# A megakernel of two conv/scan layers: loads at the head of each stage, empty half units behind them, and one more in each turn of the chunk scan

## The chip, the cores and the metric

The kernel runs on one core of one Trainium2 chip, as one launch with one instruction stream per engine: PE (TensorE, matmuls), DVE (VectorE), ACT (ScalarE), POOL (GpSimd) and SP (SyncE, which here issues every DMA). The metric is device time in microseconds. The time of the kernel before is the median of three runs.

## The reference

Eight images of 64 x 64 tokens with 192 channels go through two layers, all in float32. Cut to what matters:

```python
# layer 0 (INNER=384, K=2 directions, N=32 states, 12 heads of 64)
xl, z = split(x @ W_in.T)                      # 384 + 384 channels
xc = silu(depthwise3x3(xl) + conv_b)
BCdt = x_proj(xc in row order, xc in column order)
dt = softplus(dt + dt_bias); da = exp(dt * A)
h = da_t * h + dt_t * x_t * B_t ; y_t = h . C_t       # over 4096 tokens, twice
y = y0 + y1 (turned back), + Ds * x
out = x + (y * silu(z)) @ W_out.T
x1 = out + silu(out @ W1.T + b1) @ W2.T + b2
# layer 1 (halves of 96 channels; inner 192, 16 states, 4 directions)
left  = relu(conv1x1(relu(bn(conv3x3(relu(bn(conv3x3(bn(xl)))))))))
u = silu(depthwise3x3(in_proj(layernorm(xr)))); four orders of the tokens
delta = softplus(dt_proj(x_dbl)); A = -exp(A_logs)
h = exp(delta_t * A) * h + delta_t * u_t * B_t ; y_t = h . C_t   # 4 directions
right = out_proj(layernorm(sum of directions + Ds * u) * silu(z))
out = interleave(left, right) + x1
```

## The kernel before

**The main sequence.** Layer 1's scan (`selective_scan`) is the backbone. A unit is one [128 x 1024] block: eight channels of one direction with their 16 states on the partitions, and 1024 tokens along the free axis. There are 3072 units, 384 per image: 8 steps of 3 tiles of 16 units. For each unit SP fetches the decays into `dA` (`fetch`, L1390, four units ahead, in five buffers, so a fetch waits until the scan five units back has let its buffer go), ACT takes the exponent (`decay`, L1395), PE spreads the inputs into PSUM (`spread`, L1403), the DVE multiplies by B (`weigh`, L1418) and scans (L1425), POOL multiplies by C (L1429), ACT keeps the last column (`carry_on`, L1435 and L1436), and every fourth unit PE sums over the states (`gather`, L1447). `prepare` computes the next tile's softplus and its inputs in pieces over the 16 units, with ACT, POOL and several DMAs (`dld`, `dud`, `dus`, L1359 to L1381).

**The work beside it.** Everything else runs as Python generators beside the scan: `conv0`, `ssd` and `mlp0` are layer 0 of the next image; `conv_branch`, with `scan_sums` as its side, and `scan_outputs` finish the image before; `scan_inputs` and `transposed` prepare layer 1's scan of the next image. `stages` lists them when an image's loop starts, at the ninth unit of the second tile in the last step of the image before.

**The order of the instructions.** All engines take their instructions in program order (`pin`), which the emitter fixes by a credit rule (class `Beside`). A unit has two halves. In each half `Beside.half` adds the rate to the credit (what is left over counts up to one more rate), and then emits pieces of the first stage in the list. A piece ends with `yield cost`, and the cost is taken off the credit; at zero the half is over. A piece that ends with `yield None` ends the half at once, whatever the credit. The costs of the stages are what their pieces yielded when the first image went through before the loop (`finish`, without the scan and without pacing), apart from two that are written down:

```python
self.rate = (own + sum(self.costs.get(gen.__name__, 40.0) for gen in self.stages)) / halves
```

`own` is 450 and `halves` is 768 for a whole image. What is left in the list when the loop of an image ends is emitted in one lump by `finish`. The side of `conv_branch` moves in every half up to its next `None`, without credit.

**The stages that the change touches.** Each stage opens its own SBUF pools when it starts and issues its first loads there. `conv0` loads its weights and x, sets three pads to zero on POOL (L371), then projects, convolves and, in `turn`, transposes into `xo` (ACT copy L440) and projects into `po`, which SP stores to `xrows` and `prows` (L461). `ssd` is the chunked scan of layer 0: `group` loads B, C and dt of eight chunks from `prows` (L512, L513) and computes their decays on POOL (L520), ACT and PE; then 32 chunks go through `fetch`, `decays` (PE turns B and C into `ps_t`, L586, and ACT copies them to `bc`, L591), `weigh`, `outputs` (the DVE adds to `Hm`, L639; POOL makes `Hn`, L641; the DVE adds to `Hn`, L654; PE multiplies `ps_y`, L664) and `store`, one stage per chunk and turn, oldest chunk first (`in_turn`). `mlp0` loads y from `yrows`, gates, projects and runs the MLP over blocks of 512 tokens. `conv_branch`, `scan_inputs` and `scan_outputs` run over blocks of 512 tokens through `in_turn`, too, with a load as the first stage. `scan_sums` adds up the directions: a whole [128 x 4096] tile, then blocks, each loaded a block ahead. `transposed` writes the turned copy of `u`.

Of the kernel before, what the change touches and what calls it, by code (L numbers as in the profile page):

```python
# [18 lines left out]
PW = WW + 2  # L19
# [269 lines left out]

def in_turn(items, *stages):  # L290
# [64 lines left out]
def conv0(cx, x):  # L355
# [3 lines left out]
    with cx.pool("cw0") as wp, cx.pool("v0", 2) as vp:  # L359
        w_in = load_split(cx, wp, "w_in", k["p0_w_in"][:, :INNER0], INNER0)  # L360
        diag = wp.tile([128, NJ, 9, 64], F32, tag="diag", name="diag")
        pin(nc.sync.dma_start(out=diag, in_=k["diag0"]))
        xp = wp.tile([128, 2 * NJ, 2 * NP0], F32, tag="xp0", name="xp0")
        for i in range(2):
            pin(nc.sync.dma_start(
                out=xp[64 * i : 64 * (i + 1)], in_=k["p0_xp"].rearrange("(j p) k m -> p j (k m)", p=64)
            ))

        pads = [wp.tile([128, R2 + 2, PW], F32, tag=f"pad{j}", name=f"pad{j}") for j in range(NJ)]
        for j in range(NJ):  # L370
            pin(nc.gpsimd.memset(pads[j], 0.0))  # L371
# [59 lines left out]
        def turn(p, q):  # L431

            here = slice(q * 128, (q + 1) * 128)
            xo = vp.tile([128, 2, INNER0], F32, tag="xo", name="xo")
# [27 lines left out]

        load(0)
        for j in range(NJ):
            yield from project(0, j)
        load(1)
# [13 lines left out]
def ssd(cx):  # L480
# [15 lines left out]
    with cx.pool("g0", 2) as gp, cx.pool("s0", 2) as sp:  # L496
# [63 lines left out]
        for _ in coming:  # L560
            yield 0.3
# [14 lines left out]
        def decays(c):  # L576
# [12 lines left out]
            yield 0.6  # L589
            bc = sp.tile([2 * N0, 2, Q], F32, tag="bc", name="bc")  # L590
# [35 lines left out]
        def outputs(c):  # L626
# [25 lines left out]
            yield 0.9  # L652
            ps = pss[1].rearrange("p (h c) -> p h c", c=HP)
            pin(nc.vector.tensor_add(Hn, ps, Hn))  # L654
            yield None
# [37 lines left out]
def mlp0(cx, x, x1):  # L693
# [9 lines left out]
    with cx.pool("mw0") as wp, cx.pool("m0", 2) as mp:  # L703
        w_z = load_split(cx, wp, "w_z", k["p0_w_in"][:, INNER0:], INNER0)
        w1 = load_split(cx, wp, "w1", k["p0_w1"], HID)
        w_out = wp.tile([128, NJ, C], F32, tag="w_out", name="w_out")
        pin(nc.sync.dma_start(out=w_out, in_=k["p0_w_out"].rearrange("(j p) m -> p j m", p=128)))
        w2 = wp.tile([128, NF, C], F32, tag="w2", name="w2")
        pin(nc.sync.dma_start(out=w2, in_=k["p0_w2"].rearrange("(f p) m -> p f m", p=128)))
# [120 lines left out]
        load_x(0)  # L830
        load_y(0)
        for i in range(NI + 1):
# [16 lines left out]
def conv_branch(cx, xl, short, out, side=None):  # L849

    nc, pin, k = cx.nc, cx.pin, cx.k
    with cx.pool("cw1") as wp, cx.pool("a1", 2) as ap:
        ws = []
        for n in ("conv1_w", "conv2_w"):
            w = wp.tile([CH, 9, CH], F32, tag=n, name=n)
            pin(nc.sync.dma_start(out=w, in_=k[n]))
            ws.append(w)
# [822 lines left out]
```

## Time and profile before

| | us |
|---|---|
| median of three runs (17870.95 to 17890.11) | 17880.6 |
| profiled execution, its own time | 17927.61 |
| its span from the first to the last instruction | 17925.8 |
| busy: PE, DVE, POOL, ACT | 13953, 12239, 12013, 10436 |
| first and last scan of the main sequence | 934.9 and 17692.4 |
| loop of an image (the third with all seven stages) | 2178 |

The profile lists groups of instructions by line: engine, operation, tiles, shape and count, then busy time, the mean of one in ns, and the idle time of that engine just before them with what ended it. The view of the waits gives, for a pair of a waiting instruction and the one that released it, the total in us, the number of times and the longest. The timeline shows instructions in order of time: start, duration, engine, line, and in brackets the idle time before. The view by windows gives busy times in a stretch. Granted clock is the share of full speed at which PE was clocked.

### The profile page before, as it was taken

Reading aid. Unit: us, or ns where it says so; the run is one execution under the profiler, and the core shown is the slowest. Engines: PE = TensorE matmul, PEld = TensorE weight load, DVE = VectorE, ACT = ScalarE, POOL = GpSimd, SP = SyncE. Lnnn points to the kernel's source line nnn. Section 1 sums busy time; section 2 is a strip of 40 time slices with the busy share of each in tenths; the row PEclk is TensorE's granted clock in tenths of the full one; section 3 lists DMA queues with packets and bytes.
Section 4 is the critical chain, followed back from the end, with each engine's and each line's share of the span. In section 5 each row is a group of like instructions: output and inputs, shape, how many; then the busy total and the mean of one; then the engine's idle time right before and its main releaser. Section 6 shows DMA issues by size and latency. Waiting matters only on the chain. (4 is left out here: it accounts for less than half of the span.)

```text
span 17925.8 us, 221564 instructions
## 1 busy us (share of the span) xinstructions
PE 13953.2 (78%) x75752; PEld 4910.9 (27%) x75752; DVE 12239.1 (68%) x9264; ACT 10435.9 (58%) x18285; POOL 12013.0 (67%) x6437
## 2 busy tenths in 40 slices
PE   8877787778877787778877788777887777878776
PEld 4423322332123321233213332133322333211111
DVE  2177777676777767677567775677756777667884
ACT  2364576465664656647566475654756547555664
POOL 4168766775668756687567865677756786567784
PEclk9987788788787887878878788787977778877676
DMA  3376777677776777767777677777777767778785
GB/s 89 95 195 168 181 187 207 163 194 185 180 202 162 199 189 176 193 171 196 186 187 187 172 196 186 186 182 177 194 182 189 183 179 196 178 199 202 193 204 142
DMA packets 1584062, 3241.99 MB, mean 181 GB/s; under 512 B 387465, under 2 KB 834073, under 8 KB 1579353
## 3 DMA queue, kind: packets, MB, share of 16 engines
q1 hardware_dynamic: 1582936, 3227.82, 70.8%
q8 instruction: 605, 9.91, 0.2%
q14 instruction: 521, 4.26, 0.1%
HBM read 2548.91 MB, written 678.18 MB: 180 GB/s over the span
## 5 line engine op out<-in xcount | busy, mean ns | idle before, releaser
L1429 POOL TENSOR_TENSOR h<-h,bc 128x1023 f32<-128x1023 f32 x3072 | 7229.4, 2357 | 4209.2 <-DVE h L1425 3592.1
L1425 DVE TENSOR_TENSOR_SCAN h<-dA,carry,dB 128x1024 f32<-128x1024 f32 x3072 | 7198.0, 2343 | 594.0 <-ACT dA L1395 187.3
L1418 DVE TENSOR_TENSOR dB<-dB,bc 128x1024 f32<-128x1024 f32 x3072 | 3741.6, 1218 | 3133.2 <-PE dB L1403 3126.0
L1395 ACT ACTIVATE dA<-dA,neg_a 128x1024 f32<-128x1024 f32 x3072 | 3487.5, 1135 | 746.1 <-DMA dA<-dld 743.5
L1447 PE MATMUL acc<-h,gather 128*32 128x512 f32 x12288 | 2476.9, 749 | 733.0 <-ACT h L1436 235.9
L1403 PE MATMUL dB<-dus,spread 24*128 24x512 bf16 x6144 | 1364.2, 432 | 437.9 <-DVE h L1425 340.0
L1452 ACT COPY y<-acc 128x512 f32<-128x512 f32 x1536 | 871.7, 576 | 1227.1 <-PE acc L1447 1225.0
L868 PE MATMUL ps_c<-p,conv_w 96*96 96x512 f32 x2304 | 1294.9, 690 | 116.3 <-ACT p L889 105.3
L1403 PEld LDWEIGHTS <-spread 24*128 24x128 bf16 x6144 | 308.0, 94 | 2682.5 <-issue 1645.6
L1436 ACT ACTIVATE h<-h,bc 128x1 f32<-128x1 f32 x3072 | 905.4, 295 | 162.6 <-ACT carry L1435 2.2
L664 PE MATMUL ps_y<-dtx,M 64*64 64x64 f32 x12288 | 758.1, 253 | 298.5 <-DVE Hn L654 291.1
L1435 ACT COPY carry<-h 128x1 f32<-128x1 f32 x3072 | 573.9, 187 | 600.7 <-DVE h L1425 598.0
L325 PE MATMUL ps_cv<-pad,diag 64*64 64x512 f32 x6912 | 847.1, 607 | 31.0 <-ACT xc L428 30.5
L1447 PEld LDWEIGHTS acc<-h,gather 128*32 128x32 f32 x12288 | 323.1, 118 | 1850.3 <-issue 929.4
L664 PEld LDWEIGHTS ps_y<-dtx,M 64*64 64x64 f32 x12288 | 635.8, 165 | 491.1 <-issue 259.7
L596 PE MATMUL ps_d<-R,after 128*128 128x384 f32 x1024 | 627.3, 706 | 111.1 <-DVE M L621 54.1
L1349 POOL TENSOR_TENSOR w<-w,e 128x1024 f32<-128x1024 f32 x192 | 452.5, 2357 | 284.0 <-ACT carry L1435 195.4
L868 PEld LDWEIGHTS ps_c<-p,conv_w 96*96 96x96 f32 x2304 | 374.9, 182 | 855.7 <-issue 717.6
L350 PE MATMUL ps_h<-oa,w1a 128*128 128x256 f32 x1536 | 483.0, 438 | 159.1 <-ACT h L810 90.0
L591 ACT COPY bc<-ps_t 64x256 f32<-64x256 f32 x256 | 93.4, 365 | 728.6 <-PE ps_t L586 726.3
L779 PE MATMUL ps_m<-h,w 128*128 128x512 f32 x768 | 436.2, 710 | 78.3 <-DVE gT L774 36.8
L654 DVE TENSOR_TENSOR Hn<-ps_s,Hn 64x384 f32<-64x384 f32 x256 | 139.9, 546 | 518.8 <-POOL Hn L641 510.2
(258 smaller groups left out, 22143.6 us busy)
## 6 DMA issues: line engine op xcount, KB each, us to landing
dA<-dld SPq DMA_DIRECT2D x3072, 512.0 KB
dud<-terms SPq DMA_DIRECT2D x192, 768.0 KB
dus<-dud SPq DMA_DIRECT2D x2304, 64.0 KB
bc<-bcd SPq DMA_DIRECT2D x256, 512.0 KB
y<-yrows SPq DMA_DIRECT2D x256, 384.0 KB
u<-u SPq DMA_DIRECT2D x192, 512.0 KB
dld<-dl SPq DMA_DIRECT2D x192, 512.0 KB
y<-y SPq DMA_DIRECT2D x3072, 32.0 KB
```

Of the source, the lines that this page charges most:

```text
L325: pin(nc.tensor.matmul(ps[64 * b : 64 * (b + 1)].rearrange("p (h w) -> p h w", w=WW), lhsT=diag[:, t, :], rhs=pad[64 * i : 64 * (i + 1), b ...
L596: pin(nc.tensor.matmul(ps, lhsT=k["after"], rhs=flat(R[:, d * NH : (d + 1) * NH, :]), start=True, stop=False))
L664: pin(nc.tensor.matmul(psy[d][here, h * HP : (h + 1) * HP], lhsT=M[here, d, h, :], rhs=dtx[here, d, h, :], start=True, stop=d == 1,))
L868: pin(nc.tensor.matmul(ps.rearrange("p (h w) -> p h w", w=WW), lhsT=w[:, t, :], rhs=pad[:, dy : dy + RB, dx : dx + WW], start=t == 0, stop ...
L1395: pin(nc.scalar.activation(dAs[q], dAs[q], AF.Exp, scale=k["neg_a"][:, steps[m][1], t, i : i + 1]))
L1403: pin(nc.tensor.matmul(dBs[q][:, half, :], lhsT=k["spread"][at : at + 3 * UD, :], rhs=du_of[n][at : at + 3 * UD, i // 2, :], start=True, s ...
L1418: pin(nc.vector.tensor_mul(dBs[q], dBs[q], of(q)[0]))
L1425: pin(nc.vector.tensor_tensor_scan(order(h, g), order(dA, g), order(dB, g), carry, ALU.mult, ALU.add))
L1429: pin(nc.gpsimd.tensor_mul(h[:, rest], h[:, rest], C_[:, rest]))
L1436: pin(nc.scalar.activation(end, end, AF.Identity, scale=C_[:, last : last + 1]))
L1447: pin(nc.tensor.matmul(ps[32 * v : 32 * (v + 1)], lhsT=k["gather"], rhs=hs[q - 3 + v][:, here], start=True, stop=True))
L1452: pin(nc.scalar.copy(y[:, here], ps))
```

## The change

All edits are to the order in which instructions are emitted or to the number of buffers:

- `conv0`, `mlp0`, `conv_branch`, `scan_inputs`: the tiles that the first pieces need are loaded first, the other weights after them, then some half units pass without pieces (`pause`), and only then are pads set to zero and work begun. `conv_branch` and `scan_inputs` now load a block two blocks ahead from inside a later stage instead of in a stage of their own.
- `ssd`: the five steps of the first group stand 8, 2, 2, 3 and 2 empty halves apart.
- `ssd`, each turn: one more empty half in `decays`, between the transposes into `ps_t` and the copy to `bc`. In `outputs` the empty half after the add to `Hn` moves in front of it.
- `scan_sums`: longer waits behind the loads of a whole tile and of the first block.
- `scan_outputs`: six empty halves behind the first load, and one stage more between load and use.
- Buffers: `xo` 3 for 2, `xt` of `scan_inputs` 5 for 4, `va` and `vb` 7 for 6.
- The rate: the stages' work is spread over 12 halves fewer for each stage in the list.

The diff, cut to its core:

```diff
@@ -287,6 +287,12 @@
+def pause(n):
+    for i in range(n):
+        yield None
@@ -357,18 +363,6 @@
     with cx.pool("cw0") as wp, cx.pool("v0", 2) as vp:
-        w_in = load_split(cx, wp, "w_in", k["p0_w_in"][:, :INNER0], INNER0)
-        diag = wp.tile([128, NJ, 9, 64], F32, tag="diag", name="diag")
-        pin(nc.sync.dma_start(out=diag, in_=k["diag0"]))
-        xp = wp.tile([128, 2 * NJ, 2 * NP0], F32, tag="xp0", name="xp0")
-        for i in range(2):
-            pin(nc.sync.dma_start(
-                out=xp[64 * i : 64 * (i + 1)], in_=k["p0_xp"].rearrange("(j p) k m -> p j (k m)", p=64)
-            ))
-        pads = [wp.tile([128, R2 + 2, PW], F32, tag=f"pad{j}", name=f"pad{j}") for j in range(NJ)]
-        for j in range(NJ):
-            pin(nc.gpsimd.memset(pads[j], 0.0))
         first = [wp.tile([n, WW], F32, tag=f"first{n}", name=f"first{n}") for n in (128, 64)]
@@ -431,7 +425,7 @@
             here = slice(q * 128, (q + 1) * 128)
-            xo = vp.tile([128, 2, INNER0], F32, tag="xo", name="xo")
+            xo = vp.tile([128, 2, INNER0], F32, tag="xo", name="xo", bufs=3)
             po = vp.tile([128, 2, 2 * NP0], F32, tag="po", name="po")
@@ -460,10 +454,24 @@
+        w_in = load_split(cx, wp, "w_in", k["p0_w_in"][:, :INNER0], INNER0)
         load(0)
+        diag = wp.tile([128, NJ, 9, 64], F32, tag="diag", name="diag")
+        pin(nc.sync.dma_start(out=diag, in_=k["diag0"]))
+        xp = wp.tile([128, 2 * NJ, 2 * NP0], F32, tag="xp0", name="xp0")
+        for i in range(2):
+            pin(nc.sync.dma_start(
+                out=xp[64 * i : 64 * (i + 1)], in_=k["p0_xp"].rearrange("(j p) k m -> p j (k m)", p=64)
+            ))
+        pads = [wp.tile([128, R2 + 2, PW], F32, tag=f"pad{j}", name=f"pad{j}") for j in range(NJ)]
+        yield from pause(8)
+        for j in range(NJ):
+            pin(nc.gpsimd.memset(pads[j], 0.0))
+        yield from pause(2)
+        load(1)
         for j in range(NJ):
             yield from project(0, j)
-        load(1)
         for p in range(NP):
@@ -557,8 +565,10 @@
         coming = group(0)
-        for _ in coming:
-            yield 0.3
+        for n in (8, 2, 2, 3, 2):
+            next(coming)
+            yield from pause(n)
+        next(coming, None)
         coming = None
@@ -587,6 +597,7 @@
             yield 0.6
+            yield None
             bc = sp.tile([2 * N0, 2, Q], F32, tag="bc", name="bc")
@@ -650,9 +661,9 @@
             yield 0.9
+            yield None
             ps = pss[1].rearrange("p (h c) -> p h c", c=HP)
             pin(nc.vector.tensor_add(Hn, ps, Hn))
-            yield None
             yo = sp.tile([128, 2, NH, HP], F32, tag="yo", name="yo")
@@ -701,12 +712,6 @@
     with cx.pool("mw0") as wp, cx.pool("m0", 2) as mp:
-        w_z = load_split(cx, wp, "w_z", k["p0_w_in"][:, INNER0:], INNER0)
-        w1 = load_split(cx, wp, "w1", k["p0_w1"], HID)
-        w_out = wp.tile([128, NJ, C], F32, tag="w_out", name="w_out")
-        pin(nc.sync.dma_start(out=w_out, in_=k["p0_w_out"].rearrange("(j p) m -> p j m", p=128)))
-        w2 = wp.tile([128, NF, C], F32, tag="w2", name="w2")
-        pin(nc.sync.dma_start(out=w2, in_=k["p0_w2"].rearrange("(f p) m -> p f m", p=128)))
         gT = wp.tile([128, 2, NJ, T], F32, tag="gT", name="gT")
@@ -828,7 +833,14 @@
         load_x(0)
+        w_z = load_split(cx, wp, "w_z", k["p0_w_in"][:, INNER0:], INNER0)
         load_y(0)
+        w_out = wp.tile([128, NJ, C], F32, tag="w_out", name="w_out")
+        pin(nc.sync.dma_start(out=w_out, in_=k["p0_w_out"].rearrange("(j p) m -> p j m", p=128)))
+        w1 = load_split(cx, wp, "w1", k["p0_w1"], HID)
+        w2 = wp.tile([128, NF, C], F32, tag="w2", name="w2")
+        pin(nc.sync.dma_start(out=w2, in_=k["p0_w2"].rearrange("(f p) m -> p f m", p=128)))
+        yield from pause(8)
         for i in range(NI + 1):
@@ -850,18 +862,9 @@
     with cx.pool("cw1") as wp, cx.pool("a1", 2) as ap:
-        ws = []
-        for n in ("conv1_w", "conv2_w"):
-            w = wp.tile([CH, 9, CH], F32, tag=n, name=n)
-            pin(nc.sync.dma_start(out=w, in_=k[n]))
-            ws.append(w)
         pads = [[wp.tile([CH, RB + 2, PW], F32, tag=f"p{c}{i}", name=f"p{c}{i}") for i in range(2)] for c in range(2)]
-        for c in range(2):
-            for i in range(2):
-                pin(nc.gpsimd.memset(pads[c][i], 0.0))
-        xs, ys, os, shs = {}, {}, {}, {}
-        cx.side = side
+        xs, ys, os, shs, ws = {}, {}, {}, {}, []
@@ -879,7 +882,6 @@
             ))
-            yield 0.0
@@ -892,6 +894,8 @@
         def first(r):
+            if r + 2 < NB:
+                load(r + 2)
             ps = cx.one("ps_c1")[:CH]
@@ -931,7 +935,19 @@
-        yield from in_turn(range(NB), load, scale, first, wait, second, third, add, store)
+        load(0)
+        for n in ("conv1_w", "conv2_w"):
+            w = wp.tile([CH, 9, CH], F32, tag=n, name=n)
+            pin(nc.sync.dma_start(out=w, in_=k[n]))
+            ws.append(w)
+        load(1)
+        cx.side = side
+        yield from pause(6)
+        for c in range(2):
+            for i in range(2):
+                pin(nc.gpsimd.memset(pads[c][i], 0.0))
+        yield from pause(1)
+        yield from in_turn(range(NB), scale, first, wait, second, third, add, store)
         while cx.aside():
@@ -985,19 +1001,16 @@
             size = c1 - c0
-            diag[n] = wp.tile([size, 9, 64], F32, tag="diag" + n, name="diag" + n)
-            pin(nc.sync.dma_start(out=diag[n], in_=k["diag_" + n]))
             pads[n] = [wp.tile([size, R2 + 2, PW], F32, tag=f"p{n}{i}", name=f"p{n}{i}") for i in range(2)]
-            for i in range(2):
-                pin(nc.gpsimd.memset(pads[n][i], 0.0))
         xs, us, sqs = {}, {}, {}
         def load(r):
-            xs[r] = bp.tile([CH, 512], F32, tag="xt", name="xt", bufs=4)
+            xs[r] = bp.tile([CH, 512], F32, tag="xt", name="xt", bufs=5)
             pin(nc.sync.dma_start(out=xs[r], in_=xr[:, r * 512 : (r + 1) * 512]))
-            yield 0.0
         def mean(r):
+            if r + 2 < NB:
+                load(r + 2)
             sqs[r] = yield from center(cx, bp, [xs[r]], [k["m96"][:CH, :CH]])
@@ -1045,7 +1058,16 @@
-        yield from in_turn(range(NB), load, mean, norm, project, wait, wait, convolve, store)
+        for r in range(2):
+            load(r)
+        for n, c0, c1 in parts:
+            diag[n] = wp.tile([c1 - c0, 9, 64], F32, tag="diag" + n, name="diag" + n)
+            pin(nc.sync.dma_start(out=diag[n], in_=k["diag_" + n]))
+        yield from pause(6)
+        for n in "ab":
+            for i in range(2):
+                pin(nc.gpsimd.memset(pads[n][i], 0.0))
+        yield from in_turn(range(NB), mean, norm, project, wait, wait, convolve, store)
@@ -1095,14 +1117,14 @@
                 pin(nc.sync.dma_start(out=whole[size:], in_=seconds[1]))
-                yield from slots(2)
+                yield from slots(4)
             else:
...
                         pin(nc.sync.dma_start(out=others[q], in_=seconds[1][:, cols(q, 512)]))
-                    yield from slots(1)
+                    yield from slots(5 if q == 0 else 1)
                     if q > 0:
@@ -1120,6 +1142,7 @@
             coming = load(0)
+            yield from slots(4)
             for r in range(NB):
@@ -1150,8 +1173,10 @@
             for n, src in (("a", y[0]), ("b", y[2][0:64])):
-                v = st[r][n] = ep.tile([src.shape[0], 512], F32, tag="v" + n, name="v" + n, bufs=6)
+                v = st[r][n] = ep.tile([src.shape[0], 512], F32, tag="v" + n, name="v" + n, bufs=7)
                 pin(nc.sync.dma_start(out=v, in_=src[:, cols(r)]))
+            if r == 0:
+                yield from pause(6)
             yield 0.0
@@ -1197,7 +1222,10 @@
-        yield from in_turn(range(NB), load, mean, norm, gate, apply, project, store)
+        def ahead(r):
+            yield 0.0
+        yield from in_turn(range(NB), load, ahead, mean, norm, gate, apply, project, store)
@@ -1211,7 +1239,9 @@
-        self.rate = (own + sum(self.costs.get(gen.__name__, 40.0) for gen in self.stages)) / halves
+        work = sum(self.costs.get(gen.__name__, 40.0) for gen in self.stages)
+        self.rate = own / halves + work / (halves - 12 * len(self.stages))
```

## The prediction

> **What bounds the kernel now.** I read the page first, then the waits, the timeline around the places where the vector engine (DVE) stands still, and last the windows by stage (the third full image loop, 7180 to 9358 us).
>
> ```profile
> span 17925.8 us, 221564 instructions
> ...
> PE 13953.2 (78%) x75752; PEld 4910.9 (27%) x75752; DVE 12239.1 (68%) x9264; ACT 10435.9 (58%) x18285; POOL 12013.0 (67%) x6437
> ...
> L1425 DVE TENSOR_TENSOR_SCAN h<-dA,carry,dB 128x1024 f32<-128x1024 f32 x3072 | 7198.0, 2343 | 594.0 <-ACT dA L1395 187.3
> L1418 DVE TENSOR_TENSOR dB<-dB,bc 128x1024 f32<-128x1024 f32 x3072 | 3741.6, 1218 | 3133.2 <-PE dB L1403 3126.0
> ```
>
> No engine is full. The 3072 scan units cost the DVE 2343 + 1218 ns each; where nothing is in the way scans start 3.60 us apart, yet the loop (934.9 to 17692.4 us) needs 5.46. The DVE's largest wait is for PE's spread (L1403), a matmul of 0.4 us: it comes late because PE takes instructions in order and stands at something else. The waits that the edits touch:
>
> ```profile
> DVE dB L1418 <- PE dB L1403: 3126.0, 873, 110.7
> ...
> ACT dA L1395 <- DMA dA<-dld: 743.5, 276, 20.9
> ACT bc L591 <- PE ps_t L586: 726.3, 189, 11.1
> ...
> DVE Hn L654 <- POOL Hn L641: 510.2, 201, 8.4
> ...
> PE ps_y L664 <- DVE Hn L654: 291.1, 118, 7.4
> ...
> ACT xo L440 <- DMA xrows<-xo: 142.8, 26, 15.7
> ```
>
> The timeline at the start of conv0 (idle time and its end in brackets):
>
> ```profile
> 7200.28 0.43 SPq L386 DMA_DIRECT2D xa<-in_x_dram  x1
> ...
> 7203.98 0.55 SPq L1390 DMA_DIRECT2D dA<-dld  x1
> ...
> 7206.30 0.66 PE L350 MATMUL ps_in<-first,w_ina 128*128 128x64 f32 x2 [18.33 <-DMA xa<-in_x_dram]
> ...
> 7216.49 1.23 DVE L1418 TENSOR_TENSOR dB<-dB,bc 128x1024 f32<-128x1024 f32 x1 [33.12 <-PE dB L1403]
> ```
>
> PE waits 18 us for a tile that SP asked for 6 us before; the spread sits behind it, and the DVE idles 33.1 us. The same happens at every start in this loop: conv0 33.1, ssd 25.8, mlp0 20.9, conv_branch 11.8, scan_sums 16.6 and 15.6, scan_outputs 12.9, scan_inputs 12.6 and 11.6: **161 us of DVE idle** in a loop of 2178.
>
> ```profile
> 7180.00:7220.00 40.00, 17.08 (x48) 6.02 (x48) 5.72 (x3) 14.45 (x22) 8.38 (x6) 0.61 0.70 188
> ...
> 7552.00:7588.00 36.00, 12.21 (x63) 6.06 (x62) 7.21 (x6) 7.27 (x20) 15.93 (x14) 0.52 0.70 148
> 7588.00:8142.00 554.00, 422.51 (x3857) 187.38 (x3855) 422.73 (x428) 248.49 (x491) 470.01 (x297) 0.76 0.67 169
> 8142.00:8174.00 32.00, 13.21 (x120) 8.46 (x118) 11.02 (x12) 6.86 (x13) 9.34 (x5) 0.72 0.85 237
> ...
> 7407.00:7455.00 48.00, 47.57 (x312) 12.85 (x304) 41.53 (x24) 40.76 (x68) 42.29 (x22) 0.95 0.69 194
> 17400.00:17690.00 290.00, 163.86 (x480) 24.52 (x480) 260.84 (x151) 162.31 (x303) 229.25 (x99) 0.62 0.74 183
> ```
>
> Columns: length, then busy us of PE, weight loads, DVE, ACT, POOL; granted clock; DMA share; GB/s. At the starts PE and DVE are both idle. In a stretch of conv0 without a stop, PE is full (47.57 of 48). In the ssd (fourth line) POOL is fullest, 85%. The last line is what a pause looks like: scan units alone.
>
> **How the change moves the schedule.** I followed the yields through the credit rule, half by half. A loop stays 384 units. Before: conv0 75, ssd 90.5, mlp0 89.5, conv_branch 55.5, scan_outputs 25.5, scan_inputs 42, transposed 6 (the timeline's stage starts agree). After: 70, 106.5, 84.5, 53, 25.5, 39.5, 5. The new rate is 450/768 + 1168/(768-84) = 2.29 credits a half instead of 2.11. The pauses take 37 halves outside the ssd, 17 at its start, 32 in its turns. Two of transposed's pieces no longer fit and are emitted in a lump by `finish`.
>
> **Starts.** A pause of 8 halves is 14.4 us of scan at the floor, about what the late loads need (ssd: `raw` is used at 7572.8, 18 us after the last store at 7554.6). What is late next is dA: its fetch stands behind the stage's loads on SP's queue. A fetch issued in unit q has until the scan five units on, 18 us. At the ssd start SP is held 8 us by prows' landing, then issues 13 loads, so the next dA leaves 18 us late and lands some 7 later: 9 us stay. At mlp0's some 3.7 MB stand in front of it; at the 237 GB/s of that row 16 us plus 3 of issue: 5 stay. conv0: 13, as transposed still holds SP with its DMAs. The others: 2 or 3 each. Left: 44 of 161; **117 us less DVE idle a loop**.
>
> **Other edits.** Hn's add moves a half later, behind one more DVE instruction of 1.2 or 2.35 us; it waits 65 us a loop on POOL, mean 2.5. Bounds: 46 less, or 10 more, since PE's ps_y queues behind Hn (291 + 174 us in all, matmuls and weight loads) and the spread behind ps_y; I take 25. The half before the bc copy: ACT is 45% busy in the ssd and its wait ends nothing there; between 0 and 10, I take 0. A third xo: 18 us a loop of ACT's wait, but po has still two buffers and its store follows xrows by 1 us, so ACT would stop there instead; 0 to 15, I take 5. Transposed's lump: two copies of 1.9 us on ACT and their DMAs ahead of the next `u` loads on SP; 2 to 12, I take 6. First image before the loop and the tail run without pauses: -10 for loads issued earlier, bounds -20 and +5.
>
> **Two sums.** If only the DVE counts (a unit costs 3.60 wherever it runs, plus idle), a loop gains 117+25+5-6 = 141. For this: from loop 0 to loop 1 the rate rose from 1.88 to 2.11 credits and no excess grew with it (conv0: 440 us in 87 units, then 369 in 75). Six loops 846, loop 0 70, loop 7 45: **961 us**.
>
> If PE bounds all but the ssd, as the full stretch says, only PE's idle counts. At the starts outside the ssd it is 102 us (22.9 and 18.8 from the rows, 60 from the timeline). Afterwards the 18.5 pause units leave PE idle 3.60-1.25 each (gather and spread: 2476.9+1364.2 over 3072), 43 us, and the leftovers 25: gain 34. 15.5 units of scan move into the ssd, where PE has room: 15.5x1.25 = 19. With xo and transposed, 52. The ssd loses: at its start 17 halves are 30.6 us plus 9, for 26 before (+14); its turns take 7.5 units more, 27, less Hn's 25 (+2). Net **36 a loop**; 216, with loop 0 (30) and loop 7, whose rate is low and which keeps its 45: **291 us**.
>
> The truth lies between, nearer PE's end, for 92 to 99% PE is what I find in most stretches without a stop: a quarter of the way up, **450 us with the outer stages**. From the profiled execution's 17927.6 that is 17478. That execution lies 47 above the median of the runs; **17430**.
>
> **A rule against the change.** The trace grants a clock of 0.61, 0.52 and 0.72 at the starts, 0.62 in scan alone, 0.95 in the full stretch. [...] by the rows the starts are already as cold, so outside the ssd I add nothing. For the 32 new halves in the ssd [...] with PE at 76% and POOL at 85% I cost it at 0[...].
>
> **Rivals.** (1) The DVE sum holds, 961 us: 16920 (20%). Against it: the full PE. (2) The pauses are too short: dA stays late behind the bursts and half of each start remains; 36 us more idle a loop, about 200 in all: 17630, from 17550 to 17830 (18%). (3) Slower: the ssd's turn. Its new half is not absorbed, since POOL has 15.7 us of work in a turn of 17.8 and the chain POOL, DVE, PE keeps its waits: a turn grows by the whole 1.8 us, 32x7x1.8 = 403. The other terms give 315; so +90, 17970, and it decides from 1.4 us a turn on. For it: the ssd took 640 us in 102.5 units and 596 in 90.5. Against: Hn's wait is attacked in the same turn (12%). No change where these cancel: 4%. My case has 46%, 17250 to 17550. A difference of 0.2% is about what can be told from none here. Range 16980 to 17850.
>
> **What would show it.** Right: the DVE's wait for dB falls from 3126 by 500 or more; the 33, 26 and 21 us gaps become 13, 9 and 5, ended by dA; Hn's wait falls below 300; the ssd lasts about 610 us a loop; conv0 and mlp0 shrink by 15 each. Wrong: ssd over 640, gaps of 20 us at starts, `u<-part` holding SP longer.

## The result and the profile after

| | before | after |
|---|---|---|
| median, us | 17885.4 (4 runs, 17870.95 to 17909.29) | 17585.3 (4 runs, 17570.44 to 17616.91) |
| ratio | | 0.9833, 95% interval 0.9816 to 0.9851 |
| profiled execution, its own time | 17927.6 | 17570.4 |
| loop of an image, mean of the same five loops | 2185 | 2135 |

The change is 300 us faster. The forecast was 17430 (450 faster), in a range from 16980 to 17850. The total is right in sign and range, and lies 35 us above the band of my own case (17250 to 17550). Behind it, two terms were mis-sized in opposite directions, one weighing failed and one loss was not seen at all; the errors partly cancel.

The page of the kernel after, in the rows that answer to those shown of before (busy us and mean ns, then the idle time just before and what ended most of it):

```profile
span 17568.6 us, 221210 instructions
...
PE 14009.8 (80%) x75752; PEld 4902.0 (28%) x75752; DVE 12282.8 (70%) x9264; ACT 10492.5 (60%) x18322; POOL 12006.7 (68%) x6437
...
L1455 DVE TENSOR_TENSOR_SCAN h<-dA,carry,dB 128x1024 f32<-128x1024 f32 x3072 | 7202.5, 2345 | 722.9 <-ACT dA L1425 246.8
L1448 DVE TENSOR_TENSOR dB<-dB,bc 128x1024 f32<-128x1024 f32 x3072 | 3746.6, 1220 | 2682.2 <-PE dB L1433 2675.1
L1425 ACT ACTIVATE dA<-dA,neg_a 128x1024 f32<-128x1024 f32 x3072 | 3489.0, 1136 | 1259.3 <-DMA dA<-dld 1256.1
```

The work has not changed: each of these groups takes as long as before (2345 ns for 2343 in the scan, 1220 for 1218 in the product, 1136 for 1135 in the exponent). The DVE's wait for the spread fell by 451 us (3126.0 to 2675.1). ACT's wait for the decays' fetch rose from 743.5 to 1256.1, and the scan's wait for those decays from 187.3 to 246.8.

The view of the waits after:

```profile
DVE dB L1448 <- PE dB L1433: 2675.1, 1039, 110.6
...
ACT dA L1425 <- DMA dA<-dld: 1256.1, 371, 22.9
...
ACT bc L602 <- PE ps_t L596: 388.8, 139, 7.4
...
DVE Hn L666 <- POOL Hn L652: 377.7, 131, 7.8
PE ps_y L675 <- DVE Hn L666: 345.8, 118, 6.7
```

The two waits that the ssd's edits aim at did shrink: `bc` from 726.3 to 388.8, `Hn` from 510.2 to 377.7. The wait behind them, `ps_y` for `Hn`, grew from 291.1 to 345.8.

The timeline at three stage starts after, ssd (begins at 7345), mlp0 (7975) and the next conv0 (9156). The bracket is the idle time just before, and what ended it:

```profile
7363.39 2.35 DVE L1455 TENSOR_TENSOR_SCAN h<-dA,carry,dB 128x1024 f32<-128x1024 f32 x1 [3.88 <-ACT carry L1465]
...
7996.02 1.15 ACT L1425 ACTIVATE dA<-dA,neg_a 128x1024 f32<-128x1024 f32 x1 [17.04 <-DMA dA<-dld]
7997.20 2.35 DVE L1455 TENSOR_TENSOR_SCAN h<-dA,carry,dB 128x1024 f32<-128x1024 f32 x1 [10.50 <-ACT dA L1425]
8006.18 1.02 DVE L779 TENSOR_TENSOR gT<-ps_t,gT 128x512 f32<-128x512 f32 x2 [6.63 <-PE ps_t L773]
...
8027.52 1.23 DVE L1448 TENSOR_TENSOR dB<-dB,bc 128x1024 f32<-128x1024 f32 x1 [9.44 <-PE dB L1433]
...
9178.41 2.35 DVE L1455 TENSOR_TENSOR_SCAN h<-dA,carry,dB 128x1024 f32<-128x1024 f32 x1 [8.14 <-ACT dA L1425]
...
9192.43 1.23 DVE L1448 TENSOR_TENSOR dB<-dB,bc 128x1024 f32<-128x1024 f32 x1 [11.68 <-PE dB L1433]
```

ssd is nearly mended: 3.9 us, and 7.2 behind the pause, in place of 25.8. At conv0 one long stop has become two: first the decays are late, then, behind the pause, the spread stands behind the stage's first real work. At mlp0 it is the same with a third stop between them, 6.6 us at mlp0's own first product `gT`. In conv_branch (begins at 8459) the stop has only moved behind the pause:

```profile
8473.88 1.15 ACT L1425 ACTIVATE dA<-dA,neg_a 128x1024 f32<-128x1024 f32 x1 [11.55 <-DMA dA<-dld]
...
8475.40 0.87 ACT L891 ACTIVATE p<-xt,bn_b,bn_g 96x576 f32<-96x576 f32 x1
...
8476.32 8.11 PE L871 MATMUL ps_c<-p,conv_w 96*96 96x512 f32 x12 [13.37 <-ACT p L891]
...
8484.79 1.23 DVE L1448 TENSOR_TENSOR dB<-dB,bc 128x1024 f32<-128x1024 f32 x1 [16.66 <-PE dB L1433]
```

ACT stands 11.6 us at a late fetch of decays. The scaled rows `p` come behind it on ACT (no bracket: they waited for nothing but their turn), the convolution (8.1 us on PE) waits for `p`, and the spread for the convolution. This is the chain of before with another first link: a load of the scan in place of a load of the stage.

Here is the account that all later readings rest on. I summed, over five whole image loops, the idle time before every DVE instruction by the stage that was running. A stage counts from its first instruction on any engine. The loop less this idle time is 1528 us before and 1535 after, the DVE's own work. That is bookkeeping, and not a proof that the DVE sets the pace: POOL's busy time is 1500 to 1502 us a loop in every kernel of this study, so the same account could be kept for POOL. The account tells in which stage time is lost. In us per loop:

| DVE idle in | conv0 | ssd | mlp0 | conv_branch | scan_outputs | scan_inputs | transposed | sum | loop |
|---|---|---|---|---|---|---|---|---|---|
| before | 105 | 164 | 119 | 154 | 40 | 63 | 11 | 657 | 2185 |
| after | 70 | 139 | **152** | 135 | 32 | 55 | 17 | 600 | 2135 |

The starts and `Hn` took idle time out of five stages. In mlp0 33 us came in, and not at its start: in the first 60 us of the stage the DVE idles 32 us (30 before), in the rest 121 (89 before). That is the first thing that the prediction does not hold.

### The profile page after: what moved, and what is told of

It reads as the page before. It is cut to its first block, busy times and chain, and to the rows that moved or that the text cites. A ratio compares the mean times of both kernels' runs of the same rounds, so it can differ in the third digit from the quotient of the medians.

```text
span 17568.6 us, 221210 instructions
## 1 busy us (share of the span) xinstructions
PE 14009.8 (80%) x75752; PEld 4902.0 (28%) x75752; DVE 12282.8 (70%) x9264; ACT 10492.5 (60%) x18322; POOL 12006.7 (68%) x6437
## 4 chain that ended last, share of the span: by engine, by line
PE 28%; DMA 19%; ACT 13%; POOL 13%; DVE 13%; issue 6%; SPq 2%; DVEq 0%; POOLq 0%; ACTq 0%
DMA dA<-dld 10%; DVE h L1455 8%; POOL h L1459 5%; PE acc L1477 4%; DVE dB L1448 4%; PE ps_c L871 3%; DMA dus<-dud 3%; PE ps_cv L331 3%; ACT dA L1425 2%; PE dB L1433 2%; PE ps_sum L1151 2%; PE ps_m L784 1%; POOL w L1379 1%; PE ps_y L675 1%; PE ps_xp L1330 1%
## 5 line engine op out<-in xcount | busy, mean ns | idle before, releaser
L1455 DVE TENSOR_TENSOR_SCAN h<-dA,carry,dB 128x1024 f32<-128x1024 f32 x3072 | 7202.5, 2345 | 722.9 <-ACT dA L1425 246.8
L1448 DVE TENSOR_TENSOR dB<-dB,bc 128x1024 f32<-128x1024 f32 x3072 | 3746.6, 1220 | 2682.2 <-PE dB L1433 2675.1
L1425 ACT ACTIVATE dA<-dA,neg_a 128x1024 f32<-128x1024 f32 x3072 | 3489.0, 1136 | 1259.3 <-DMA dA<-dld 1256.1
L1477 PE MATMUL acc<-h,gather 128*32 128x512 f32 x12288 | 2541.7, 753 | 836.0 <-POOL h L1459 276.3
L1433 PE MATMUL dB<-dus,spread 24*128 24x512 bf16 x6144 | 1404.2, 442 | 532.4 <-DVE h L1455 437.9
L675 PE MATMUL ps_y<-dtx,M 64*64 64x64 f32 x12288 | 813.1, 264 | 355.0 <-DVE Hn L666 345.8
L1465 ACT COPY carry<-h 128x1 f32<-128x1 f32 x3072 | 574.1, 187 | 444.4 <-DVE h L1455 440.4
L675 PEld LDWEIGHTS ps_y<-dtx,M 64*64 64x64 f32 x12288 | 677.4, 175 | 553.1 <-issue 235.1
L607 PE MATMUL ps_d<-R,after 128*128 128x384 f32 x1024 | 564.0, 640 | 204.7 <-DVE M L632 122.7
L1330 PE MATMUL ps_xp<-u,xp 128*108 128x512 f32 x768 | 484.2, 721 | 110.4 <-DMA u<-u 91.1
L681 PE MATMUL ps_y<-X,skip 64*64 64x64 f32 x6144 | 504.9, 262 | 0.0
L1400 POOL TENSOR_TENSOR terms<-du,terms 128x1024 bf16<-128x1024 f32 x192 | 409.3, 2132 | 139.3 <-ACT terms L1398 139.3
```

The costliest lines, as they stand in the source:

```text
L675: pin(nc.tensor.matmul(psy[d][here, h * HP : (h + 1) * HP], lhsT=M[here, d, h, :], rhs=dtx[here, d, h, :], start=True, stop=d == 1,))
L1330: pin(nc.tensor.matmul(ps[:NXP], lhsT=k["xp"][:, g, t, :], rhs=u_of[m][t][:, here], start=t == 0, stop=t == 2))
L1425: pin(nc.scalar.activation(dAs[q], dAs[q], AF.Exp, scale=k["neg_a"][:, steps[m][1], t, i : i + 1]))
L1433: pin(nc.tensor.matmul(dBs[q][:, half, :], lhsT=k["spread"][at : at + 3 * UD, :], rhs=du_of[n][at : at + 3 * UD, i // 2, :], start=True, s ...
L1448: pin(nc.vector.tensor_mul(dBs[q], dBs[q], of(q)[0]))
L1455: pin(nc.vector.tensor_tensor_scan(order(h, g), order(dA, g), order(dB, g), carry, ALU.mult, ALU.add))
```

## The experiments

Each run was measured beside the kernel before on the same chip, in five rounds; ratios are to that kernel. Runs 1 to 4, 5 to 8, 9 to 11 and 12 were four such sets on four chips. The kernel before had medians from 17873 to 17894 in them, so a difference in us between runs of different sets, or to the change, is uncertain by some 20.

### 1. The new rate alone, on the kernel before

```diff
-        self.rate = (own + sum(...)) / halves
+        self.rate = own / halves + work / (halves - 12 * len(self.stages))
```

> The kernel before with one line of the change: the new rate (2.30 credits a half instead of 2.11), no pauses, no moves. The same work is packed into fewer halves, and by the credit rule the last stage of a loop ends at unit 332.5 instead of 361, so 28.5 units of each full loop run without side work. Theory P (PE bounds the stages outside the ssd, so packing gives no time back): the free units leave PE idle 2.3 us each, 66 us in each of six full loops and some 25 in the first, about 420 us slower, 18300. Theory D (the DVE's units and the stalls are all that counts, packing is free): no change, 17885 +- 40. Between them, as the prediction took it (a quarter of the way from P): about 300 slower.

Measured: 17951.4, ratio 1.0041 (1.0028 to 1.0055), 72 us slower. By the count of yields the stages end 28.5 units before the next list starts, and those units then run without side work. How long they took there was not read; scan units alone at the end of the kernel before started 3.87 us apart on average (76 of them from 17398.48 to 17688.8 us). The loop took 2191 us, 6 more than before. The stages themselves got shorter (conv0 from 369 to 334 us a loop, mlp0 from 462 to 437, conv_branch from 359 to 317). If PE were full everywhere outside the ssd, squeezing its work into fewer units would stretch each of these by as much as the freed units save, and leaving PE idle in the freed ones would be lost whole. It nearly balances, so PE is not the bound that the lower of my two sums made of it. This run also moves the later stages in the loop, which turns out to matter (runs 9 to 11); how much of the 72 us that is was not parted.

### 2. The change without the half in the ssd's turn, at rate 8

```diff
             yield 0.6
-            yield None
             bc = sp.tile(...)
-        ... work / (halves - 12 * len(self.stages))
+        ... work / (halves - 8 * len(self.stages))
```

> The changed kernel without the extra empty half in front of the copy to bc in each turn of the chunk scan; the rate takes 8 halves for each stage instead of 12, so that a loop still ends at the same unit. By the credit rule the ssd then has 96.5 units instead of 106.5, and the other stages ten more. Theory S (the ssd's turn pays for the half: the ssd went from 595 to 626 us, and its turn is 1 us longer): faster by 50 to 120 us. Theory A (the half is free or a gain, since ACT's wait for ps_t fell from 726 to 389 us and ten units more in the packed stages are not needed): slower by 50 to 150 us. If scan units cost the same everywhere: within 40 us.

Measured: 17180.8, ratio 0.9607 (0.9593 to 0.9621), 404 us faster than the change. This is the fastest kernel of the study. At first sight the turn's half is the culprit.

### 3. The change with `Hn`'s half put back behind the add

```diff
             yield 0.9
-            yield None
             pin(nc.vector.tensor_add(Hn, ps, Hn))
+            yield None
```

> The changed kernel with one empty half of the ssd's outputs moved back behind the add to Hn, as in the kernel before. The number of halves stays. The prediction's term (25 us a loop from Hn's wait): 175 slower. From the two traces, where Hn's wait on POOL fell by 132 us and ps_y's waits on Hn rose by 56: about 80 slower. Rival (the wait only changes its place): within 30 of the changed kernel.

Measured: 17871.7, ratio 0.9995 (0.9986 to 1.0005). One moved half in the turn is worth 286 us, nearly the whole net gain. By the trace every stage begins in the same unit as in the change, so nothing else moved. The waits of this kernel:

```profile
ACT carry L1465 <- DVE h L1455: 847.7, 365, 10.0
...
DVE Hn L665 <- POOL Hn L652: 769.1, 221, 8.7
```

`Hn` waits twice as long as after the change (377.7), and the scan queues behind it on the DVE, which shows as ACT's `carry` waiting for the scan (440.4 after the change). The account says the same: the DVE idles 182 us a loop in the ssd here, 139 after the change, and in every other stage as much as there to within 3 us.

### 4. The loads of conv0 and mlp0 spread out between shorter pauses

```diff
         load_y(0)
+        yield from pause(4)
         w_out = ...
+        yield from pause(2)
         w1 = load_split(...)
+        yield from pause(2)
         w2 = ...
-        yield from pause(8)
```

(conv0 likewise: 4 halves, `diag`, 2 halves, `xp`, 2 halves.)

> The changed kernel with the same number of pauses, but the late weights inside them: in mlp0 w_out after 4 empty halves, w1 after 2 more, w2 after 2 more; in conv0 diag after 4, xp after 2 more, then 2. Theory B (what is left at a start is dA queued behind a burst of loads on SP and the DMA rings: 10.5 and 9.4 us of DVE idle at mlp0, 8.1 and 11.7 at conv0 in the changed kernel): the gaps at these two starts fall to 5 or less, 15 to 25 us a loop, 100 to 170 us faster. Rival (dA is late because of SP's block on the stores and on dud and dus, not because of these bytes): within 40.

Measured: 17587.9, ratio 0.9834 (0.982 to 0.9849), the same as the change. The waits of this kernel, and its stop at the same mlp0 start (begins at 7979) in the timeline:

```profile
ACT dA L1429 <- DMA dA<-dld: 1277.5, 382, 20.4
...
DVE h L1459 <- ACT dA L1429: 184.2, 72, 6.1
```

```profile
7996.17 2.35 DVE L1459 TENSOR_TENSOR_SCAN h<-dA,carry,dB 128x1024 f32<-128x1024 f32 x1 [4.51 <-ACT dA L1429]
...
8034.73 1.23 DVE L1452 TENSOR_TENSOR dB<-dB,bc 128x1024 f32<-128x1024 f32 x1 [15.59 <-PE dB L1437]
```

The scan waits 63 us less for the decays in all (246.8 after the change), and mlp0's stop of 10.5 us at them has shrunk to 4.5. The stop at `gT` has grown from 6.6 to 7.9 and that at the spread from 9.4 to 15.6. What one wait gave the next ones took: the bursts do make the decays late here, but mending that alone does not shorten the kernel.

### 5. The starts alone: as run 2, with `Hn`'s half back

> The loads in front and the pauses at the starts of the stages alone: the changed kernel without the half in each turn, with the half of Hn where it was, and with 8 instead of 12 in the rate. If the parts add up, the kernel without the turn's half (17181) plus what Hn's half was worth in the changed kernel (17872 - 17585 = 287): 17468, 410 faster than before. The prediction's sum over the DVE's idle (116 us a loop from starts, xo and transposed, without Hn) would give about 17090; its sum over PE (35 a loop or less) about 17650.

Measured: 17374.8, ratio 0.9711 (0.9688 to 0.9733). Loads first, pauses and a rate of 8 give 498 us without either edit in the ssd's turn. Against run 2, `Hn`'s half is worth 194 here; all stages begin in the same units as there.

### 6. The change without the turn's half, its rate 12 kept

```diff
             yield 0.6
-            yield None
             bc = sp.tile(...)
```

> The kernel without the turn's half, but with the rate of the change (12 halves for each stage, 2.29 credits instead of 2.23): by the credit rule the loop's stages then end at unit 354.5 and 6.5 units run alone. It parts the two edits of the experiment before, which gained 404 us. Theory H (the half itself costs): 17181 plus what packing cost on the kernel before (72 us for 0.19 credits, so 26 for 0.07): 17180 to 17230. Theory R (the rate costs; mlp0 took 476 us at 2.29 and 452 at 2.23, 24 in each of seven loops): 17340 or more, and mlp0 at 470 us.

Measured: 17588.3, ratio 0.9839 (0.9819 to 0.9859), the same as the change. So run 2's reading falls: taking the half away gains nothing at this rate. What differs from run 2 is the rate, and with it where each stage begins in the loop.

### 7. The turn's half alone, on the kernel before (rate 4, so that the stages still fit)

```diff
             yield 0.6
+            yield None
             bc = sp.tile(...)
-        self.rate = (own + sum(...)) / halves
+        self.rate = own / halves + work / (halves - 4 * len(self.stages))
```

> The kernel before with the turn's half alone (and 4 halves for each stage in the rate, so that the loop ends at the same unit; 2.17 credits). Theory H (a turn is longer by a half, 32 turns in 7 loops, 1.8 us each, and nothing is given back elsewhere): 300 to 400 slower, 18180 to 18280. Theory D (a unit costs the same wherever it runs; ACT's wait for ps_t, 726 us before, is shorter): 17800 to 17900. If the half only hurts together with Hn's moved half: 17900 to 18000.

Measured: 17983.2, ratio 1.0055 (1.0038 to 1.0071), 110 slower. The ssd takes 638 us a loop in place of 593, but the loop only 2188 in place of 2185: the other stages give the time back, and most of the 110 us lies outside the five loops (16 of the 64 us between the two profiled executions fall into them). This run shifts the later stages as well (mlp0 begins 8 units later), so it neither isolates the half's own price nor bounds it.

### 8. Loads first, but no pause anywhere (without the turn's half, at the old rate)

```diff
 def pause(n):
-    for i in range(n):
-        yield None
+    yield from ()
```

> The kernel without the turn's half and with every pause empty: the loads stand in front as in the change, in its order, Hn's half is moved, the longer waits in scan_sums stay, and the rate is that of the kernel before. Theory W (the pauses do the work, the order of the loads alone gives little): 17500 to 17600, about what Hn's half (287) and the waits in scan_sums give. Theory O (the order of the loads is most of the gain): 17200 to 17300.

Measured: 17412.3, ratio 0.9737 (0.9717 to 0.9756). The order of the loads, with `Hn`'s half, `xo`'s buffer and scan_sums' longer waits, gives 461 of the 698 us of run 2. By the trace all its stages begin in the same units as in the kernel before, so no place has moved in this comparison. Its DVE idle time is 73 us a loop below before's: 22 in the ssd, 19 in scan_inputs, 12 in conv0, 11 to 12 in conv_branch, 8 in mlp0.

Which starts the order mends alone shows in the DVE's idle time in the first 60 us from a stage's first load, a mean over the five loops:

| | conv0 | ssd | mlp0 | conv_branch |
|---|---|---|---|---|
| before | 36 | 34 | 30 | 24 |
| run 8, order without pauses | 36 | 35 | 23 | 21 |
| the change, with pauses | 24 | 19 | 32 | 28 |

The order alone helped mlp0 a little; conv0 and ssd needed the pauses.

### 9 to 11. The same stages at other places in the loop

A stage's place can be moved without touching it. Run 9 is run 6 with conv0's first pause 14 halves long in place of 8, run 10 with 21. Run 11 is run 2 at rate 10.

```diff
-        yield from pause(8)
+        yield from pause(14)
         for j in range(NJ):
             pin(nc.gpsimd.memset(pads[j], 0.0))
```

> The version without the turn's extra half unit at rate 12 (measured 17588), with conv0's first pause 14 half units instead of 8, so that every later stage falls six half units later against the chunk scan's turns; the rate of half units is the same 2.294. Theory A (where the stages fall against the scan's tiles decides: mlp0 then starts at unit 146.5, where it stood in the run at 17181): 17200 to 17350, mlp0 back from 477 to about 450 us a loop, outputs from 172 to about 150. Theory R (the packing at the higher rate itself costs): 17550 to 17630, mlp0 stays 470 or more. Six more half units of pause in conv0 cost nothing by either, or at most 15 us.

> The same with conv0's first pause 21 half units: all later stages about 12 half units later than in the version at rate 12 (mlp0 from unit 150.5, outputs from 290). Theory A: a time of its own, between 17200 and 17650, that differs from the run with pause 14 by over 60 us in one direction or the other. Theory R: 17550 to 17630, within 50 us of the run with pause 14.

> The version without the turn's extra half unit (measured 17181 at rate 8) at rate 10, midway to the rate 12 that measured 17588. Theory R: midway, 17340 to 17430. Theory A: no reason to lie midway; mlp0 starts at unit 145 and ends at 231.5, as near to the slow version (142.5 to 228.5) as to the fast one (146.5 to 233.5), outputs begin at 286 (282.5 in the slow one): anywhere from 17180 to 17600, and mlp0's time in the loop and not a uniform stretch of all stages carries the difference.

Measured: 17278.2, ratio 0.966 (0.9645 to 0.9675); 17563.5, ratio 0.9827 (0.9814 to 0.984); 17394.7, ratio 0.9725 (0.9711 to 0.9739). Six more empty halves in conv0 make the kernel 310 us faster; seven more on top take 285 of it away again. The rate is the same in all three, and more pause cannot be cheaper and then dearer by itself. conv0, which got the pause, idles 9 us a loop more in run 9 than in run 6. So the place decides. Run 11 lies midway, which both theories allow.

mlp0 in the same loop of run 6 and of run 9, by windows (length, then busy us of PE, weight loads, DVE, ACT and POOL; clock; DMA share; GB/s). Run 6:

```profile
12242.50:12722.30 479.80, 384.10 (x1660) 160.39 (x1660) 328.19 (x235) 349.82 (x565) 296.25 (x133) 0.85 0.69 180
```

Run 9:

```profile
12050.40:12500.90 450.50, 373.29 (x1660) 157.53 (x1660) 327.83 (x234) 338.11 (x551) 303.26 (x137) 0.88 0.74 194
```

The same 1660 matmuls and the same 328 us on the DVE, and 29 us less time. Run 10's mlp0 in the same loop, 12232.2 to 12702.2, takes 470 us again, at the clock of run 9:

```profile
12232.20:12702.20 470.00, 372.87 (x1672) 155.69 (x1672) 333.90 (x237) 341.26 (x558) 301.92 (x136) 0.88 0.72 186
```

The DVE's waits in those windows, run 6:

```profile
DVE dB L1447 <- PE dB L1432: 105.1, 33, 8.6
DVE gT L778 <- PE ps_t L772: 14.1, 3, 8.3
DVE h L1454 <- ACT dA L1424: 11.4, 2, 10.6
```

Run 9:

```profile
DVE dB L1447 <- PE dB L1432: 83.9, 41, 6.7
DVE h L1454 <- ACT dA L1424: 14.6, 5, 9.1
DVE gT L778 <- DMA dA<-dld: 6.1, 1, 6.1
```

Run 10:

```profile
DVE dB L1447 <- PE dB L1432: 104.4, 42, 8.8
```

It is the spread again: from run 6 to run 9 more waits, but each shorter (2.0 us on average against 3.2), and from run 9 to run 10, at the same clock, the wait grows by 20.5 us and the time by 19.5. I read this as fewer of the same PE pieces standing in front of the spread just when the DVE needs it; which ones they are was not followed.

### 12. The change itself, with sixteen halves of pause taken out ahead of the ssd's turns

```diff
-        yield from pause(8)
+        yield from pause(0)
         for j in range(NJ):
             pin(nc.gpsimd.memset(pads[j], 0.0))
...
-        for n in (8, 2, 2, 3, 2):
+        for n in (0, 2, 2, 3, 2):
```

> The change itself, its turn's half and its rate 12 kept, but with sixteen half units of pause taken out ahead of ssd's turns (conv0's first eight, and the first eight of ssd's first group). By a count of the work units mlp0 and everything behind it then fall as in the run at 17278 (mlp0 from unit 147, conv_branch to 286, scan_outputs to 311) instead of 11 units after the slowest place, where the change has them (153.5 to 238). Theory A, place decides and the turn's half itself costs only its own 110 to 130 us: 17280 + 120 + 0 to 70 for the eight microseconds a loop that each lost pause may let come back, so 17400 to 17480; mlp0 back from 476 to 450 to 455 us a loop while ssd stays at 610 to 630. Rival, the turn's half spoils what follows it wherever it falls: 17550 to 17650, mlp0 stays at 470 or more.

Measured: 17246.4, ratio 0.9642 (0.9615 to 0.9669), 339 us faster than the change, with the turn's half and rate 12 both in. That is below what either theory gave. The interval overlaps run 9's (no half in the turn), and by the trace conv_branch and all behind it begin in the same units as there. But run 9 has those sixteen halves of pause, and six more: the half in the turn and the lost pauses together cost nothing that I can tell from none. The waits of this kernel:

```profile
DVE dB L1448 <- PE dB L1433: 2414.7, 974, 109.8
DVE Hn L666 <- POOL Hn L652: 337.0, 143, 6.3
```

`Hn` waits about as after the change; the wait for the spread is 260 us shorter.

The runs in order of mlp0's place. The unit at which mlp0 begins is counted from the yields by the credit rule, from the image's first unit; the stages are listed 23 units before it (7 of the tile then running and 16 of the next), so that conv0 and ssd, 70 and 106.5 units long after the change, end at 153.5. The decays that SP has fetched before mlp0's first load give the same whole units in all traces. Its time runs to the next stage's start, a mean over the five loops, as is the loop:

| kernel | rate | mlp0 from unit | mlp0, us | loop, us | median, us |
|---|---|---|---|---|---|
| run 6 | 2.294 | 142.5 | 484 | 2146 | 17588 |
| run 11 | 2.259 | 145 | 472 | 2108 | 17395 |
| run 9 | 2.294 | 146.5 | 455 | 2090 | 17278 |
| run 2 | 2.226 | 146.5 | 452 | 2070 | 17181 |
| run 12 | 2.294 | 147 | 454 | 2083 | 17246 |
| run 10 | 2.294 | 150.5 | 476 | 2130 | 17564 |
| the change | 2.294 | 153.5 | 484 | 2135 | 17585 |

It is a valley a few units wide. It holds for kernels with mlp0's pause and rates near 2.26: before and run 8, without pause at the old rate, begin mlp0 at 142.5 and take 462 and 457 us for it. By the code a loop is 384 units, a multiple of the scan's tile of 16, so a stage meets the same pieces of a tile's preparation in each loop; a bad meeting would be paid every time, and the stage times do repeat (mlp0 after the change, from its first instruction to its last: 477.8, 476.5, 476.6, 474.5 and 474.5 us in five loops). mlp0 is not alone in it. From run 6 to run 9 the DVE's idle time falls by 57 us a loop: 25 less in mlp0, 19 in conv_branch, 14 each in scan_outputs and transposed and 6 in the ssd, against 22 more in scan_inputs and conv0. From run 9 to run 10 it rises by 40: 14 in the ssd, 13 in scan_inputs, 12 in mlp0, 10 in conv_branch and 1 in conv0, against 10 less in scan_outputs and transposed. So the table tells where mlp0 stood, and not that mlp0 alone decides.

## Why the prediction was right, and where it was not

**The total.** 17585 is outside the band of my own case and inside that of the second rival, 17550 to 17830: pauses too short, decays late, half of each start left. That rival reckoned with 36 us a loop more idle time at starts than I left, and 41 more were found (below), so on the starts it was right and my case wrong. It has no place in it either, which weighs more (run 9); that the sum fell this near to both is luck. Of the signs that I named, the wait for the spread fell by 451 us (I said 500 or more), `Hn`'s wait fell to 377.7 (below 300), and the ssd takes 627 us (about 610): each moved the way I named and missed the figure.

**What bounds the kernel.** Right: the DVE's largest wait was for a spread that stands behind other work in PE's order, and it is where the time came from (−451).

**Starts, "117 us less DVE idle a loop".** Mis-sized. In the loop from 7025 to 9156 the stops at starts are 6.6 and 11.0 in conv0, 3.9 and 7.2 in ssd, 10.5 and 9.4 in mlp0, 16.7 in conv_branch, 12.3 and 7.8 in scan_sums: 85 us (92 with the 6.6 at `gT`), where I left 44. So about 70 to 76 went, not 117. I was right that the decays are late next, and at the ssd (9 forecast, 3.9 found, and 7.2 behind the pause). I had not counted the second stop: late decays hold ACT too (17.04 us at mlp0, 11.55 in conv_branch), ACT hands its pieces late to PE, and in conv_branch PE's first work behind the pause is one piece of 8.11 us. At mlp0 I had blamed the 3.7 MB of loads in front of the fetch; spacing them cut the stop at the decays from 10.5 to 4.5, and nothing of the time (run 4).

**`Hn`'s half, "I take 25".** Too low. Run 3's loop is 46 us longer than the change's, with 43 us more DVE idle in the ssd: my bound, not my value. Over the kernel it is 286 us in the change, and 194 at rate 8 without the turn's half (run 5 against run 2). The wait itself fell by only 132 from before to after; what I did not reckon is that beside the turn's new half the old order would have made `Hn` wait 769.

**The half in front of the copy to `bc`, "I take 0".** Run 12 tells nothing against 0, with pauses taken out beside it; run 7's 110 has a shift of the later stages in it. The slower rival had the turn right and the loop wrong: from run 6 to the change, which differ by this half alone, the ssd grows from 580 to 627 us a loop, 1.5 us in each of 32 turns (it said 1.8), but the loop goes from 2146 to 2135. The other stages, now at other places, gave it back. The ssd's 627 us a loop lie between my 610 and the 640 that would have made the rival right.

**The two sums, "nearer PE's end".** This weighing failed, although the total (300) lies at the PE sum's 291. Run 1 packs PE's work into fewer units and costs 72 us, where the PE sum's argument asks for about 420. Runs 2, 9 and 12 are 698, 597 and 648 us faster than before; the PE sum allowed the change 291, and a turn without the half, by its own terms (52 less 14, plus `Hn`'s 25, in six loops, and the outer 75), about 450. So PE does not bound the stages outside the ssd in the way that it assumed. That does not make the DVE sum right: its 961 us had the starts too large and nothing for the place.

**What the prediction lacked: the place.** I counted after's stages unit by unit (70, 106.5, 84.5, ...) and used only their lengths. Where they begin against the scan's tiles is worth 310 us between run 6 and run 9, more than the whole change brought, and up to 339 in the change itself (run 12). I forecast conv0 and mlp0 to shrink by 15 us each; conv0 lost 52 and mlp0 gained 22. An undersized `Hn`, oversized starts and an unseen loss by place brought the total within 155 us of the forecast by compensation, not by insight.

**The clock.** For the 32 new empty halves I costed a lower clock in the ssd at 0. Before, the clock was 0.76 behind the ssd's start (7588 to 8142) and 0.75 with the start (7562 to 8149). The ssd after the change, by windows:

```profile
7346.00:7974.00 628.00, 463.72 (x4068) 199.95 (x4060) 490.77 (x469) 294.59 (x579) 537.37 (x332) 0.75 0.71 175
```

0.75 with its start, and 0.76 behind it (7390 to 7970), as before: the clock did not drop, so the 0 stands. That a lower clock would have been covered there was my estimate from PE at 76% and POOL at 85%, and is not shown. POOL is still the fullest engine there (86%).

**Third `xo`.** The trace after shows it moved as I feared: ACT no longer waits for `xrows`, and its copy to `po` now waits 63.5 us for `prows`, which it did not before. The 142.8 became 63.5. No run isolates its worth.

**Open.** Why 146.5 to 147 is good and 142.5 or 150.5 bad is not settled piece by piece. Which piece of mlp0 and of the scan's `prepare` meet there was not tried, and run 12 also takes pause out of the ssd itself, whose time fell from 627 to 594, so not all of its gain need be place. Run 9, which adds pause and gains nearly as much, is the clean one.

## What to carry to other kernels

When independent work is interleaved with a backbone by a fixed schedule, every edit that adds or drops a slot also shifts all that follows; compare such an edit with a version in which dummy slots restore the old place, or a gain of one step will be booked as a loss of another. Read the idle time of the backbone's engine by stage, over whole loops: with that engine's own work it adds up to the loop, and a stage that gained idle time away from where it was edited, as mlp0 did behind its start, is a hint that the place changed. The traces tell which comparisons are free of it: count the backbone's units before each stage's first load. After a load-first edit with a pause, look behind the pause: the stop may have moved there.

## What the runs showed of the hardware

In mlp0's windows PE's busy time followed the granted clock: the same 1660 matmuls of mlp0 took 384.10 us at 0.85 and 373.29 us at 0.88 (products 326 and 328). So 11 of the 29 us that run 9 saved there came with PE's own matmuls being shorter by the profile. Another loop of run 9 shows the same: PE was busy with 1660 matmuls for 379.28 us at 0.86 (7850 to 8309), product 326. A lower clock is not all that a bad place costs, though: run 10's mlp0 had run 9's 0.88 and took 19.5 us longer. Whether less waiting raises the clock, or a higher clock shortens the waits, is not shown.
